# Divided queries and a column of ones in two attentions, and a stream of nine chains on GpSimd and ScalarE in the tail

## The chip, the cores and the metric

The kernel runs on one core of a Trainium2 chip. The metric is the device time of one execution in microseconds; lower is better. The engines are TensorE (PE in the profile; its weight loads are PEld), VectorE (DVE), ScalarE (ACT), GpSimd (POOL) and SyncE (SP), which issues most of the transfers.

## The reference

Four images of 256 channels and 64 x 64 pixels pass four layers, all in float32. Each layer adds its result to its input and begins with a group norm (folded into weights here).

- Layer 0: a pointwise convolution, a depthwise convolution that gives offsets and masks, a deformable sampling of 36 points a pixel (bilinear, from a padded table), a projection, a squeeze-and-excite gate and a feed-forward part of 1024 hidden channels.
- Layer 1: multi-scale linear attention. The part that matters:

```python
qkv = relu(conv1x1(x) * scale + bias)               # 768 channels
agg = conv1x1_dw(conv5x5_dw(qkv))                   # 25 taps a channel
q, k, v = split(concat(qkv, agg))                   # heads of 8 channels; q, k through relu
vk = einsum('bhdn,bhen->bhde', v, k)
out = einsum('bhde,bhen->bhdn', vk, q)
denom = einsum('bhe,bhen->bhn', k.sum(-1), q)
out = out / (denom + EPS)
out = relu(conv1x1(out, proj_w) * scale + bias)
```

- Layer 2: a 3 x 3 convolution with binarised weights, 256 to 256 channels.
- Layer 3: attention whose keys and values come from a 2 x 2 max pool (1024 of them) and whose queries are all 4096 pixels:

```python
m1 = softmax(theta1 @ phi1, axis=2)                 # 4096 x 1024
m2 = m1 @ gi1                                       # 4096 x 128
out = conv1x1(m2, wz_w) + wz_b + x
```

## The kernel before

`run` goes through the images in a pipeline. The sampling of layer 0 is the backbone: `sample(n)` runs 288 rounds for each image, and in each round GpSimd issues four indirect transfers (L591), each of which gathers 256 values for each of 128 partitions into a buffer g of which there are seven. PE multiplies them with the weights wm (L598; wm is made by VectorE at L582), ScalarE copies the accumulator acc to at (L603), PE transposes it (L608), and ScalarE spreads the result (L618).

Beside those rounds a planner, `beside`, advances other generators. Each generator yields the costs of its steps, has a total, and is advanced so that its share of the total follows the share of the rounds. Beside the sampling of image n run the feed-forward part and the linear attention of image n-1 (`feed`, `linear`), and, from n = 2 on, the convolution and the pooled attention of image n-2 (`second`). Within `ordered()` each engine keeps the order in which the program emits instructions; elsewhere a scheduler decides it. After the last sampling comes the tail, where `self.alone` is true: first the feed-forward part, the linear attention of the last image and most of `second(2)`, over 900 planned steps; then the convolution of the last image with the rest of `second(2)`; then the pooled attention of the last image with wider use of PSUM.

Linear attention (`layer1`). `rows` multiplies the qkv weights (L805) in three passes over the image and writes padded rows. There are 24 "chains" an image, each a 5 x 5 depthwise convolution of 128 channels by 16 rows: `aggregate` runs one on VectorE as 25 taps of 128x1024 (L180 for the first, L178) that add up in PSUM; `products` runs one as 25 multiplies on ScalarE (L193, L196 for the first) and 24 additions on GpSimd (L194), with three buffers m between them. `chains` hands the chains out in pairs, ak and av. In the tail chains are taken in threes: the first and the third go to VectorE, the second runs beside them through `aside`, one step in every second tap. `step` is called after each tap in the tail (after every third elsewhere) and runs one closure of the list `later`, which holds all the small steps of the attention. When the last keys and values are in, `summed` masks their products to blocks of 8 (`ln`, L873). `output` makes the denominators (`dens`, L889 to L892), and for each of 8 combinations of half and channel tile `head` multiplies ln with the query (num, L898), spreads the reciprocal denominator over partitions (rden, L901), copies num to ot on ScalarE (L903) and multiplies on VectorE (L904). `proj` multiplies ot with the projection pw (L910), and relu, addition and statistics follow (L912, L913, L110). The constants LINEAR and LAST are the totals that the planner takes for `linear` beside the sampling and in the tail.

The convolution (`layer2`) subtracts and adds its inputs into xd (L987, on GpSimd in the tail), and its products are L1036.

Pooled attention (`layer3`). For each of 32 tiles of 128 queries: two products s (L1135), their maxima mx (L1136, L1137), exp on ScalarE with the sums as a second output (L1142), the sum of the two sums and its reciprocal on VectorE (L1144, L1145), eight transposes (L1150) copied by ScalarE (L1151), eight products with the values gt (L1155), and the scaling by the reciprocal on VectorE into m2 (L1156). Every four tiles a product with ww and the additions follow (L1161 to L1163).

Of the kernel before, what the change touches and what calls it, by code (L numbers as in the profile page):

```python
# [40 lines left out]
FEED = NB * 40 + 8  # L41
LINEAR, LAST = 930, 620
STEPS = 900
# [28 lines left out]
class Net:  # L72
# [675 lines left out]
    def layer1(self, n, st, st2):  # L748
# [3 lines left out]
        with tc.tile_pool(name=f"la{n}", bufs=1, side="right") as sp, \  # L752
# [13 lines left out]

            later, count, aside = [], 0, None
            room = lambda bufs, more=1: bufs + more * self.alone

            def step(cost, chains=False):  # L770


                nonlocal count
                count += chains
                if later and (not self.alone or count % 2 or not chains):
                    later.pop(0)()
                if chains:
                    if count % 8 == 6 if self.alone else count in LEADS:
                        next(made, None)
                    if count % 2 and aside:  # L780
                        next(aside, None)
                return cost
# [59 lines left out]
            def outer(t, kind, kv, vv, first, last):  # L842
# [12 lines left out]
                def added(i):  # L855
                    for j in range(2):
                        nc.tensor.matmul(sums[:, t, kind], kts[i][:, 0, j], kts[i][:, 1, j],
                                         start=first and i + j == 0, stop=last and i + 1 == len(at) and j == 1,
                                         skip_group_check=True)
# [9 lines left out]
            def summed(t):  # L869

                for kind in range(2):
                    j = 2 * kind + t
                    nc.vector.tensor_tensor(ln[:, j], sums[:, t, kind], self.con("bd"), ALU.mult)  # L873
                    kk = sp.tile([P, 1], F32, name=f"kk{j}")
                    nc.vector.tensor_reduce(kk, ks[t][:, kind, 0:(NB, NCH)[kind]], AX.X, ALU.add)
                    for h in range(2):
                        nc.vector.tensor_scalar(ld[:, j, h, 16 * h:16 * h + 16], self.con("oh"), kk, None, ALU.mult)

            def output(c, qp, aq):
# [14 lines left out]
                def head(h, j):  # L894
                    if not j:
                        xv.append(self.block(bp, self.x3_d[n], 2 * c + h, "xq", bufs=1))
                    pn = self.ps("num")
                    nc.tensor.matmul(pn, ln[:, j], qh[h][j], start=True, stop=True)  # L898
                    hs, i = slice(64 * (j // 2), 64 * (j // 2) + 64), 2 * h + j % 2
                    pb = self.ps("rden")  # L900
                    nc.tensor.matmul(pb, self.con("sel")[hs, i * P:(i + 1) * P], rd[0][hs], start=True, stop=True)  # L901
                    ot[h, j] = bp.tile([P, 512], F32, name="ot", tag="kt", bufs=4)
                    nc.scalar.copy(ot[h, j], pn)  # L903
                    nc.vector.tensor_tensor(ot[h, j], ot[h, j], pb, ALU.mult)  # L904

# [46 lines left out]
            def chain():  # L952

                while not (args := next(every)):
                    yield step(3)
                return args

            while number < 6 * NCH:
                count = 0 if not self.alone and number % 2 == 0 else count
                *args, more = yield from chain()  # L960
                if self.alone:

                    *slow, smore = yield from chain()
                    aside = products(*slow, **smore)
                    yield from aggregate(*args, **more)
                    *args, more = yield from chain()
                    yield from aggregate(*args, **more)
                    while next(aside, None):
                        pass
                    number += 3  # L970
                else:
                    yield from aggregate(*args, **more)
                    number += 1
            while later:
# [76 lines left out]
    def layer3(self, n, st, wide=False):  # L1051
        nc, tc, a = self.nc, self.tc, self.a
        M = HW // 4
        with tc.tile_pool(name=f"na{n}", bufs=1, side="left") as sp, \
# [31 lines left out]
            ph = sp.tile([P, M], F32, name="ph")  # L1086
            gt = sp.tile([P, 8, P], F32, name="gt")
            def first(b):
# [15 lines left out]
            def then(b, xq):  # L1104
# [5 lines left out]
                nc.scalar.activation(ph[:, b * P:(b + 1) * P], ps[:, 0:P], AF.Identity, bias=fb)  # L1110
                nc.vector.tensor_tensor(gt[:, b], ps[:, P:2 * P], gb, ALU.add)

# [10 lines left out]
            for b in range(NB):  # L1123
                m2 = bp.tile([P, 512], F32, name="m2")
                for j in range(4):
# [13 lines left out]
                    pe = bp.tile([P, M], F32, name="pe")  # L1139
                    den = bp.tile([P, 3], F32, name="den3")  # L1140
                    for i in range(2):
                        nc.scalar.activation(pe[:, i * 512:(i + 1) * 512], s[i], AF.Exp, bias=mx[:, 2:3], accum_out=den[:, i:i + 1])  # L1142
                    yield 2
                    nc.vector.tensor_tensor(den[:, 2:3], den[:, 0:1], den[:, 1:2], ALU.add)  # L1144
                    nc.vector.reciprocal(den[:, 2:3], den[:, 2:3])  # L1145
                    pT = bp.tile([P, 8, P], F32, name="pT")
# [7 lines left out]
                    for m in range(8):  # L1154
                        nc.tensor.matmul(ps[:, 0:P], pT[:, m], gt[:, m], start=m == 0, stop=m == 7)  # L1155
                    nc.vector.tensor_scalar(m2[:, j * P:(j + 1) * P], ps[:, 0:P], den[:, 2:3], None, ALU.mult)  # L1156
                    yield 3
# [173 lines left out]
```

## Time and profile before

| | |
|---|---|
| three runs | 7739.69, 7744.90, 7749.79 us, median 7744.9 us |
| profiled execution | 7735.88 us, with a span of 7734.1 us |
| mean granted TensorE clock | 0.851 |
| busy of the span: PE, PEld | 5939.0 us (77%), 3468.1 us (45%) |
| busy of the span: VectorE, ScalarE, GpSimd | 5191.6 us (67%), 2200.4 us (28%), 5026.2 us (65%) |
| first and last start of a gather (L591) | 133.2 us, 6250.0 us |
| first and last start of an addition of a chain on GpSimd (L194) | 6549.7 us, 7251.5 us |

A row of the profile gives line, engine, operation, output from inputs and the count; behind the bar come busy time and mean duration of one in ns, and after a second bar the time that the engine sat idle just before such instructions and what ended most of it. A row of waits gives the waiting engine and its operation, what it waited for, the total in us, how many times, and the longest. A matmul in float32 leaves two records. Matmul durations overlap, so their sum is more than the time that PE is held.

### The profile page before, as it was taken

How to read it: one execution, taken by the hardware profiler on the slowest of the kernel's cores; microseconds unless marked ns; L12 is line 12 of the kernel's file. 1: busy time of each engine (PE TensorE's matmuls, PEld its weight loads, DVE VectorE, ACT ScalarE, POOL GpSimd, SP SyncE). 2: the span in 40 equal slices, each digit the busy share in tenths (PEclk: the TensorE clock that was granted, in tenths of full speed). 3: DMA queues.
4: the chain of work that ended last, by engine and by line, in shares of the span. 5: the costliest groups of instructions: out<-in, count | busy, mean ns of one | idle time of the engine just before them, and what ended most of it. 6: DMA issues, size and time to landing. Idle time of an engine off the chain costs nothing. (4 is left out here: it accounts for less than half of the span.)

```text
span 7734.1 us, 94959 instructions
## 1 busy us (share of the span) xinstructions
PE 5939.0 (77%) x36000; PEld 3468.1 (45%) x36000; DVE 5191.6 (67%) x6665; ACT 2200.4 (28%) x4879; POOL 5026.2 (65%) x4870
## 2 busy tenths in 40 slices
PE   5666666579766677898777778987777889967899
PEld 2333333334333333446544434465444435744487
DVE  6555553644787887238888892289888933999634
ACT  1111111212222222223233222222333323655415
POOL 2777777777777777777777667777776621966220
PEclk7676776779777778999898899998888999978999
DMA  6564664565544444555544455465444432210121
GB/s 188 152 178 137 172 173 139 160 183 157 162 122 125 125 141 132 165 151 163 149 144 133 122 154 165 136 170 157 142 134 128 123 123 65 75 52 33 63 87 58
DMA packets 744344, 1031.45 MB, mean 133 GB/s; under 512 B 354128, under 2 KB 459984, under 8 KB 742352
## 3 DMA queue, kind: packets, MB, share of 16 engines
q0 software_dynamic: 221184, 604.27, 27.2%
q1 hardware_dynamic: 522704, 421.10, 18.2%
q8 instruction: 285, 4.67, 0.3%
q14 instruction: 171, 1.40, 0.1%
HBM read 856.39 MB, written 168.61 MB: 133 GB/s over the span
## 5 line engine op out<-in xcount | busy, mean ns | idle before, releaser
L591 POOL DMA_INDIRECT g<-tab,sl x4608 | 4492.3, 975 | 1757.4 <-issue 1273.2
L178 DVE SCALAR_TENSOR_TENSOR agg<-pad,vec,agg 128x1024 f32<-128x1024 f32 x2280 | 2934.0, 1287 | 60.6
L598 PE MATMUL acc<-g,wm 128*32 128x128 f32 x18432 | 1266.6, 319 | 1241.6 <-ACT at L603 711.0
L598 PEld LDWEIGHTS acc<-g,wm 128*32 128x32 f32 x18432 | 623.2, 121 | 1927.9 <-ACT at L603 951.2
L1036 PE MATMUL ps<-xd,w 128*128 128x256 f32 x3072 | 712.3, 385 | 7.3 <-DVE x L1016 2.8
L582 DVE TENSOR_TENSOR wm<-con,sl 128x768 f32<-128x768 f32 x384 | 365.8, 953 | 420.3 <-PE acc L598 400.7
L1036 PEld LDWEIGHTS ps<-xd,w 128*128 128x128 f32 x3072 | 577.6, 193 | 107.3 <-issue 29.8
L618 ACT COPY dT<-dp 64x128 f32<-64x128 f32 x1152 | 296.7, 258 | 1044.3 <-PE dp L608 705.6
L730 PE MATMUL ps<-x2f,f 128*128 128x512 f32 x1024 | 479.0, 615 | 4.0 <-ACT f L705 4.0
L740 PE MATMUL ps<-hm,f 128*128 128x512 f32 x1024 | 462.0, 600 | 0.0
L715 DVE SCALAR_TENSOR_TENSOR hm<-ps,vec,lk 128x512 f32<-128x512 f32 x256 | 192.2, 751 | 400.4 <-ACT lk L732 397.3
L805 PE MATMUL ps<-xr,qw 128*128 128x512 f32 x768 | 450.7, 718 | 11.5 <-DVE ot L904 4.1
L987 POOL TENSOR_TENSOR xd<-xp 128x640 f32<-128x640 f32 x64 | 79.5, 1269 | 477.3 <-ACT xp L999 382.9
L603 ACT COPY at<-acc 128x256 f32<-128x256 f32 x576 | 214.4, 372 | 490.0 <-PE acc L598 477.9
L732 ACT ACTIVATE lk<-ps,low 128x512 f32<-128x512 f32 x256 | 175.9, 687 | 594.9 <-PE ps L730 593.6
L631 PE MATMUL po<-dT,ow 128*128 128x288 f32 x1024 | 312.2, 455 | 13.4 <-ACT dT L626 6.5
L608 PE MATMUL dp<-ident,at 128*128 128x128 f32 x1152 | 267.6, 320 | 66.8 <-ACT dT L618 54.7
L194 POOL TENSOR_TENSOR ak<-ak,m 128x1024 f32<-128x1024 f32 x96 | 228.1, 2376 | 131.0 <-ACT m L193 126.7
L1155 PEld LDWEIGHTS ps<-gt,pT 128*128 128x128 f32 x2048 | 278.5, 215 | 60.7 <-issue 34.3
L1155 PE MATMUL ps<-gt,pT 128*128 128x128 f32 x2048 | 291.0, 302 | 7.1 <-ACT pT L1151 7.0
L730 PEld LDWEIGHTS ps<-x2f,f 128*128 128x128 f32 x1024 | 191.3, 194 | 230.1 <-issue 216.9
L194 POOL TENSOR_TENSOR av<-av,m 128x1024 f32<-128x1024 f32 x96 | 226.9, 2363 | 101.1 <-ACT m L193 96.7
(246 smaller groups left out, 7723.0 us busy)
## 6 DMA issues: line engine op xcount, KB each, us to landing
g<-tab,sl POOLq DMA_INDIRECT x4608
x<-x SPq DMA_DIRECT2D x128, 512.0 KB
xr<-x SPq DMA_DIRECT2D x96, 512.0 KB
tab<-xo SPq DMA_DIRECT2D x192, 128.0 KB
x<-in_x SPq DMA_DIRECT2D x32, 512.0 KB
y<-yc SPq DMA_DIRECT2D x32, 512.0 KB
yb<-y SPq DMA_DIRECT2D x64, 256.0 KB
x<-yb SPq DMA_DIRECT2D x64, 256.0 KB
```

Of the source, the lines that this page charges most:

```text
L178: nc.vector.scalar_tensor_tensor(to, s, wt, acc, ALU.mult, ALU.add)
L194: nc.gpsimd.tensor_tensor(acc, acc, m, ALU.add)
L582: nc.vector.tensor_tensor(wm, self.con("own").unsqueeze(1).unsqueeze(1).to_broadcast(sh), blocks[b][:, r:r + WR, G:].unsqueeze(3).to_broad ...
L591: nc.gpsimd.indirect_dma_start(out=g[:, i, :], out_offset=None, in_=table, in_offset=bass.IndirectOffsetOnAxis(ap=sl.bitcast(I32)[:, r, i: ...
L598: nc.tensor.matmul(acc[32 * i:32 * i + 32, :], wm[:, r4, 4 * i + 2 * x:4 * i + 2 * x + 2, :], g[:, i, x * P:(x + 1) * P], start=x == 0, st ...
L618: nc.scalar.copy(dT[b][hs, :, r:r + UR], dp[u][hs, :, :, s, :].rearrange("p v g o -> p g v o"))
L631: nc.tensor.matmul(po[m][:, 0:BR * OB], self.ow[:, k, m * P:(m + 1) * P], dT[b][:, k].rearrange("p r o -> p (r o)"), start=k == 0, stop=k ...
L730: nc.tensor.matmul(ps, f1[:, k, m * P:(m + 1) * P], x2[:, k], start=k == 0, stop=k == KT - 1)
L740: nc.tensor.matmul(ps, f2[:, k, m * P:(m + 1) * P], hm[:, k], start=k == 0, stop=k == 4 * KT - 1)
L805: nc.tensor.matmul(ps, qw[:, k, m * P:(m + 1) * P], x[:, k], start=k == 0, stop=k == KT - 1)
L1036: nc.tensor.matmul(ps[:, e], w[:, k, t, 2 * half + e, m * P:(m + 1) * P], v[:, 2 * half + e, k, t:t + 8], start=i % 6 == 0, stop=i % 6 == 5)
L1155: nc.tensor.matmul(ps[:, 0:P], pT[:, m], gt[:, m], start=m == 0, stop=m == 7)
```

## The change

It has four parts. In linear attention the two matrices that the query passes, ln and the projection, are multiplied once in `summed` (comb), the product takes the place of pw, and `head` divides the query itself: num and its copy are gone. In pooled attention the values get a 129th column of ones, so that the product gives the sums of the exponentials too; exp has no second output, VectorE takes the reciprocal from the product's last column, and ScalarE does the scaling. In the tail nine of 24 chains, not eight, go to GpSimd and ScalarE, as a stream of their own (`others`) that takes the next chain whenever it has ended one and advances 9/15 of a step for each tap on VectorE. LAST is 580 for 620.

```diff
-LINEAR, LAST = 930, 620
+LINEAR, LAST, ASIDE = 930, 580, 9
...
                 if chains:
                     if count % 8 == 6 if self.alone else count in LEADS:
                         next(made, None)
-                    if count % 2 and aside:
-                        next(aside, None)
+                    if aside:
+                        due += ASIDE / (6 * NCH - ASIDE)
+                        while due > 1:
+                            next(aside, None)
+                            due -= 1
                 return cost
...
-                        nc.tensor.matmul(sums[:, t, kind], kts[i][:, 0, j], kts[i][:, 1, j],
+                        nc.tensor.matmul(sums[:, t, kind], kts[i][:, 1, j], kts[i][:, 0, j],
...
             def summed(t):
 
+                pc = self.ps("comb").rearrange("p (e o) -> p e o", e=2)
                 for kind in range(2):
...
+                for kind in range(2):
+                    nc.tensor.matmul(pc[:, kind], ln[:, 2 * kind + t], pw[:, 2 * kind + t], start=True, stop=True)
+                    nc.vector.tensor_copy(pw[:, 2 * kind + t], pc[:, kind])
...
-                    pn = self.ps("num")
-                    nc.tensor.matmul(pn, ln[:, j], qh[h][j], start=True, stop=True)
...
-                    nc.scalar.copy(ot[h, j], pn)
-                    nc.vector.tensor_tensor(ot[h, j], ot[h, j], pb, ALU.mult)
+                    nc.vector.tensor_tensor(rw(ot[h, j]), qh[h][j], rw(pb), ALU.mult)
...
+            def others():
+
+                for _ in range(ASIDE):
+                    while not (args := next(every)):
+                        yield
+                    *args, more = args
+                    yield from products(*args, **more)
+
+            if self.alone:
+                aside, number = others(), ASIDE
             while number < 6 * NCH:
                 count = 0 if not self.alone and number % 2 == 0 else count
                 *args, more = yield from chain()
-                if self.alone:
-
-                    *slow, smore = yield from chain()
-                    aside = products(*slow, **smore)
-                    yield from aggregate(*args, **more)
-                    *args, more = yield from chain()
-                    yield from aggregate(*args, **more)
-                    while next(aside, None):
-                        pass
-                    number += 3
-                else:
-                    yield from aggregate(*args, **more)
-                    number += 1
+                yield from aggregate(*args, **more)
+                number += 1
+            if aside:
+                for _ in aside:
+                    pass
...
-            gt = sp.tile([P, 8, P], F32, name="gt")
+            gt = sp.tile([P, 8, P + 1], F32, name="gt")
+            nc.vector.memset(gt[:, :, P:], 1.0)
...
-                    den = bp.tile([P, 3], F32, name="den3")
                     for i in range(2):
-                        nc.scalar.activation(pe[:, i * 512:(i + 1) * 512], s[i], AF.Exp, bias=mx[:, 2:3], accum_out=den[:, i:i + 1])
+                        nc.scalar.activation(pe[:, i * 512:(i + 1) * 512], s[i], AF.Exp, bias=mx[:, 2:3])
                     yield 2
-                    nc.vector.tensor_tensor(den[:, 2:3], den[:, 0:1], den[:, 1:2], ALU.add)
-                    nc.vector.reciprocal(den[:, 2:3], den[:, 2:3])
...
-                        nc.tensor.matmul(ps[:, 0:P], pT[:, m], gt[:, m], start=m == 0, stop=m == 7)
-                    nc.vector.tensor_scalar(m2[:, j * P:(j + 1) * P], ps[:, 0:P], den[:, 2:3], None, ALU.mult)
+                        nc.tensor.matmul(ps[:, 0:P + 1], pT[:, m], gt[:, m], start=m == 0, stop=m == 7)
+                    rden = bp.tile([P, 1], F32, name="rden")
+                    nc.vector.reciprocal(rden, ps[:, P:P + 1])
+                    nc.scalar.activation(m2[:, j * P:(j + 1) * P], ps[:, 0:P], AF.Copy, scale=rden)
```

More of the change, by code (lines that the diff above doesn't have):

```diff
@@ L765, in layer1 @@
             nc.vector.memset(ld, 0.0)
-            later, count, aside = [], 0, None
+            later, count, aside, due = [], 0, None, 0
             room = lambda bufs, more=1: bufs + more * self.alone
             def step(cost, chains=False):
-                nonlocal count
+                nonlocal count, due
                 count += chains
@@ L1110, in then @@
                 nc.scalar.activation(ph[:, b * P:(b + 1) * P], ps[:, 0:P], AF.Identity, bias=fb)
-                nc.vector.tensor_tensor(gt[:, b], ps[:, P:2 * P], gb, ALU.add)
+                nc.vector.tensor_tensor(gt[:, b, 0:P], ps[:, P:2 * P], gb, ALU.add)
             xq = None
```

## The prediction

> **What bounds the kernel now.** I read the share of each engine first, then the 40 slices, then busy times by stretch, then who waits in each stretch, and last the groups of single stretches.
>
> ```profile
> POOL 2777777777777777777777667777776621966220
> L591 POOL DMA_INDIRECT g<-tab,sl x4608 | 4492.3, 975 | 1757.4 <-issue 1273.2
> L178 DVE SCALAR_TENSOR_TENSOR agg<-pad,vec,agg 128x1024 f32<-128x1024 f32 x2280 | 2934.0, 1287 | 60.6
> ```
>
> GpSimd is level at 7 until slice 32. Those are the 4608 gathers of the sampling: 0.95 us each and 0.30 us of issue ("issue" 318.4 us over 1045 times in the third image), so 1.25 us, and 1152 of them for an image are 1440 us. Up to 6258 us the gathers set the time, unless they are held up. The waits of GpSimd for PE, by image (second, third, fourth; from the waits of 1540:3040, 3000:4620 and 4600:6258), say where they are:
>
> ```profile
> POOL g L591 <- PE acc L598: 21.0, 16, 4.6
> ...
> POOL g L591 <- PE acc L598: 119.4, 72, 7.6
> ...
> POOL g L591 <- PE acc L598: 114.1, 67, 6.7
> ```
>
> In the second image linear attention alone runs beside the sampling and little is lost. In the third and fourth the convolution and the pooled attention of an earlier image run too, and about 98 + 93 us are lost. Most of it lies where pooled tiles and the output of linear attention overlap. Below are two stretches of the third image, then the tail (columns: stretch, length, busy PE, PEld, DVE, ACT, POOL):
>
> ```profile
> 3860.00:4240.00 380.00, 269.31 (x2179) 183.96 (x2178) 337.17 (x407) 136.94 (x339) 280.20 (x293) 0.88 0.48 138
> 4240.00:4560.00 320.00, 247.13 (x1605) 142.39 (x1604) 272.57 (x334) 100.07 (x241) 199.07 (x207) 0.87 0.42 123
> ...
> 6548.00:6775.00 227.00, 216.60 (x1040) 175.78 (x1040) 217.84 (x245) 142.72 (x190) 201.79 (x98) 0.99 0.25 69
> 6775.00:7000.00 225.00, 149.00 (x596) 100.78 (x595) 214.81 (x259) 132.94 (x198) 144.81 (x61) 0.80 0.15 49
> 7000.00:7253.00 253.00, 200.26 (x674) 106.27 (x673) 235.74 (x277) 137.35 (x207) 138.75 (x60) 0.89 0.12 40
> 7253.00:7345.00 92.00, 83.67 (x330) 46.81 (x330) 39.02 (x83) 35.46 (x69) 0.86 (x1) 0.99 0.21 73
> 7345.00:7530.00 185.00, 182.94 (x863) 159.04 (x862) 55.88 (x124) 25.71 (x38) 39.56 (x32) 1.00 0.31 92
> 7530.00:7734.00 204.00, 190.00 (x1040) 145.17 (x1040) 94.69 (x253) 103.35 (x232) 0.00 (x0) 0.98 0.17 57
> ```
>
> In 4240:4560 a gather takes 320/207 = 1.55 us; VectorE is busy 85%, PE 77%. From 6548 to 7253 VectorE is busy 668.4 of 705 us: the tail's linear attention is bound by VectorE, its first third by PE too (216.6 of 227). From 7253 on PE bounds.
>
> ```profile
> L1144 DVE TENSOR_TENSOR den<-den 128x1 f32<-128x1 f32 x21 | 20.9, 997 | 0.0
> L1156 DVE TENSOR_SCALAR m<-ps,den 128x128 f32<-128x128 f32 x21 | 7.2, 345 | 0.8 <-PE ps L1155 0.8
> ...
> L194 POOL TENSOR_TENSOR ak<-ak,m 128x1024 f32<-128x1024 f32 x96 | 228.1, 2376 | 131.0 <-ACT m L193 126.7 <-DVE agg L178 0.6
> L194 POOL TENSOR_TENSOR av<-av,m 128x1024 f32<-128x1024 f32 x96 | 226.9, 2363 | 101.1 <-ACT m L193 96.7
> L987 POOL TENSOR_TENSOR xd<-xp 128x640 f32<-128x640 f32 x26 | 32.5, 1271 | 0.0
> ```
>
> These are groups of 6548:7253. An add of one element a partition (L1144) takes 997 ns there, though its median over the run is 154.
>
> **What the Trainium skill says.** "SBUF — State Buffer", section "SBUF: two separate sides": VectorE with two SBUF inputs and a GpSimd operation that reads SBUF share a port pair as an exclusive lock held for the whole instruction. The 997 ns beside GpSimd's 2.37 us adds, and about 147 ns beside the gathers (2.20 us for 15 in 4240:4560), agree. "GPSIMD Engine Reference", section 4.1, calls GpSimd about 2x slower on two-input operations: here 2.37 us against VectorE's 1.287 us for a tap, 1.84x, with ScalarE's multiply (L193, 1157 ns) on top. "TensorE: Matmul & The Clock Gate", section "Architectural detail", has ACT and DVE as strict first-in-first-out: an operation that waits holds all behind it. The trace agrees: in 4240:4560 ScalarE waits 55.6 us for mx of L1137, and PE 49.1 us for ScalarE's copies at L603.
>
> **The change, part by part.**
>
> *Divided queries.* For each of 128 heads (32 an image) the product num (two matmul records of 0.43 us of PE, the pace of L910 on the timeline) and ScalarE's copy (586 ns) go; VectorE's multiply (680 ns) stays and takes the query for the copy. So PE loses 27.5 us an image, ScalarE 18.8, VectorE nothing. In exchange pw is multiplied by ln once: four comb products an image (0.43 us each for two records, at half the width) and four copies of 128x256 (423 ns, as L1019). VectorE waits for PE between them; bounds 0.5 us (the hop) to 5 us (PE waiting for a gather), I take 1. Behind it wait taps; in the second to fourth images' sampling VectorE has room for that at this point, in the tail it costs about 6 us with the copies. No DMA and no SP instruction is added or moved in number.
>
> *Column of ones.* For each of 32 tiles an image VectorE loses the den add and the scaling (345 ns) and keeps a reciprocal, now from PSUM (164 ns from SBUF; bounds 150 to 350). ScalarE loses two accumulator reads (197 ns each) and gains the scaling of 128x128 from PSUM (368 ns, the row of L1110): about even. The product gets 129 columns for 128: 1.78 us a tile becomes 1.794. A slower odd width can't be excluded; bound 10%, 6 us in the last stage. The new wait: ScalarE's scaling waits for VectorE's reciprocal, and behind it on ScalarE are the at copies, exp, and the multiplies for GpSimd.
>
> *Sampling.* In 4240:4560 VectorE loses 15 x (0.147 + 0.345) = 7.4 us, PE 32 x 0.43 = 13.8, ScalarE 9.4. Of VectorE's 47 us idle I take 8 to go, as its waits for rden, ps and pr (31 us) stand behind shorter PE work. That gives 15 us of the 61 above 207 x 1.25. In 3860:4240 only 14 us are above 293 x 1.25, and 16 x 0.5 = 8 us leave VectorE: 5. The fourth image repeats the third, the first and second gain nothing (gathers cover it): **-40 us**; bounds 0 and -110, and below nothing by the rival on ScalarE.
>
> *Tail, nine of 24 chains.* VectorE loses a chain, 24 x 1.284 + 1.336 = 32.2 us, and in 6548:7253 21 den adds (20.9) and 21 scalings (7.2): 60.3, less 6 for comb: 54. GpSimd gains 24 x 2.37 = 57 us: 455 + 57 + 32.5 = 545 of some 660, still under VectorE; ScalarE 29 + 7.7 - 12.9 - 8.7 = +15. GpSimd's chain adds now stand up to six, not five, ahead of each pair of xd (L987), at most 2.4 us more for the convolution, which works a block ahead: nothing. The instruction order has 148 taps on VectorE, not 159, before the last statistics of conv(2): 11 of the 25 removed taps, 14 us, fall where PE is the bound too, and I count 5 of them. 54 - 9 = 45, and 5 off for ScalarE and GpSimd out of step: **-40 us**; bounds -60 and 0.
>
> *7253 to 7345.* Ten num products leave PE (8.6 us), but 13 heads instead of 11, and 8 additions at L913 instead of 6, come after the last tap: **-3**. *Last stage:* 0.5 us for the columns; in the new PE order, about a dozen times only the product (1.78 us) stands between the second half of s and the transposes that need its exp (2.75 before), and that chain takes 1.91 on the timeline: 1.6 us; at the very end VectorE and ScalarE for VectorE alone, 0.3: **+3** rounded, up to +10. conv(3), 7345 to 7530, is PE's and unchanged.
>
> Sum: -40 - 40 - 3 + 3 = **-80 us**, from the profiled execution's 7735.9 to 7656. The median of the runs shown is 9 us above that execution, so 7744.9 - 80 = **7665 us**.
>
> **Rivals.**
>
> *ScalarE waits for rden (slower).* Place: 64 tiles beside the gathers and 21 in the tail. For: VectorE runs behind there, and the like wait for mx costs ScalarE 55.6/15 = 3.7 us a tile. Against: ScalarE has just been brought level with VectorE by mx, and seven gather buffers lie between PE and GpSimd. It decides above (80 + 15)/85 = 1.1 us a tile; at half of 3.7 it costs 157 us: 7744.9 + 77 = **7822 us**. 9%.
>
> *Half lands.* In the tail GpSimd, busy 89% already in 6548:6775, becomes the bound with ScalarE (gain 0 to 10), or the sampling is held by PE's waits for at and keeps its 40. For: 0.6 GpSimd steps a tap need 1.42 us beside 1.28. Against: other VectorE work of over 0.4 us a tap. **7705 us**, 20%.
>
> *More lands.* The gather waits of the third and fourth image fall by 110 rather than 40, and the tail gives 55: **7580 us**. For: a queue just over its limit (1.25 us a gather against 272.6/207 = 1.32 of VectorE) frees up steeply. Against: convolution and group norm lose there too and are untouched. 14%.
>
> *It does not do what it says.* VectorE still multiplies every head, so "lighter" touches engines with room, and the ninth chain only moves the bound: within 15 us of **7745 us**, 5%. Against: taps of VectorE in the tail are 375 for 400 in the instruction order.
>
> **How the numbers follow.** The forecast case has 52%, its own range is 7630 to 7695. With most of "half" and half of "more" the range is 7600 to 7730; left out are the slower rival, part of no change and the far end. A change of 0.2%, 15 us, is about what a measurement of this kernel can tell from none: faster 0.52 + 0.20 + 0.14 = 0.86, same 0.05, slower 0.09.
>
> **What would show it.** Right: waits of L591 for acc in the third and fourth images near 100 us each; the chain stage some 665 us long with VectorE over 93% busy and GpSimd about 545 us; last stage 204 to 210 us. Wrong: ScalarE waiting over 1 us a tile for rden with PE's wait for at longer; GpSimd over 95% in the chain stage; the tile's product above 1.9 us.

## The result, and the profile after

The changed kernel takes 7822.6 us (median of four runs, 7819.5 to 7826.5), the kernel before 7746.4 us (four runs, 7739.7 to 7749.8): **slower, ratio 1.0097 [1.0084, 1.0110], +76 us**. 7665 us was forecast, with a range from 7600 to 7730 us.

The profiled span is 7817.7 us for 7734.1. From the page of the changed kernel (the slices of GpSimd, then two groups: busy us, mean ns, idle before):

```profile
POOL 2777777777777777767777667777776612976220
...
L591 POOL DMA_INDIRECT g<-tab,sl x4608 | 4506.5, 978 | 1785.2 <-issue 1263.5
L178 DVE SCALAR_TENSOR_TENSOR agg<-pad,vec,agg 128x1024 f32<-128x1024 f32 x2257 | 2904.0, 1287 | 61.2
```

GpSimd idles longer before its gathers (1785 us for 1757), and a gather is as long as it was: nothing was gained in the sampling. The taps on VectorE are fewer, as meant, by 30 us. The waits of the second image, then of the third, then of the fourth (total us, times, longest):

```profile
POOL g L591 <- PE acc L598: 21.6, 19, 4.6
...
POOL g L591 <- PE acc L598: 138.4, 79, 11.3
ACT m L1162 <- DVE rden L1161: 134.8, 32, 15.3
...
ACT pe L1148 <- DVE mx L1144: 89.4, 22, 7.8
...
POOL g L591 <- PE acc L598: 132.5, 80, 8.9
ACT m L1162 <- DVE rden L1161: 132.0, 32, 12.9
```

The gathers wait 138 and 132 us for PE in the third and fourth images, where before they waited 119 and 114 and where 100 was to show the forecast right. The new wait of ScalarE for rden is 267 us over 64 tiles, 4.2 us a tile. By stretches (length, busy PE, PEld, DVE, ACT, POOL, granted clock): two stretches beside the gathers, the chain stage, the output after the last tap, the convolution, and the last stage:

```profile
3860.00:4240.00 380.00, 268.78 (x2152) 182.38 (x2152) 327.69 (x372) 136.00 (x318) 280.32 (x288) 0.87 0.47 136
4240.00:4560.00 320.00, 235.72 (x1498) 137.44 (x1498) 256.78 (x295) 90.99 (x204) 194.46 (x201) 0.84 0.41 120
6545.00:7309.00 764.00, 591.01 (x2414) 406.03 (x2412) 639.32 (x770) 450.19 (x613) 545.39 (x246) 0.86 0.18 55
7309.00:7405.00 96.00, 82.66 (x285) 42.60 (x284) 37.29 (x62) 28.99 (x47) 4.91 (x3) 0.95 0.16 55
7405.00:7605.00 200.00, 190.01 (x885) 164.33 (x884) 57.14 (x131) 29.78 (x41) 39.52 (x32) 0.97 0.32 97
7605.00:7818.00 213.00, 194.02 (x1043) 145.98 (x1041) 81.36 (x189) 107.30 (x200) 0.00 (x0) 0.97 0.16 55
```

VectorE, GpSimd and PE all work less in 4240:4560, yet 201 gathers pass in it for 207. In the chain stage VectorE is busy 639 of 764 us, 84%, where over 93% was forecast: it lost work and waits instead. GpSimd's 545 us are as forecast.

To compare kernels I cut each span at the same events: the last gather, the last matmul of the feed-forward part (L740), VectorE's last tap, the last relu of the projection, the convolution's last matmul, and the end of the span (us):

| kernel | last gather | feed | chain | output | convolution | last stage |
|---|---|---|---|---|---|---|
| before | 6250.0 | 255.7 | 747.1 | 78.7 | 197.9 | 204.7 |
| after | 6292.0 | 253.2 | 764.2 | 96.3 | 199.4 | 212.6 |
| e1 divided queries | 6272.2 | 254.2 | 738.8 | 75.3 | 199.0 | 206.2 |
| e2 column, ScalarE scales | 6291.1 | 257.2 | 733.7 | 79.1 | 202.0 | 212.9 |
| e8 column, VectorE scales | 6256.2 | 255.7 | 741.1 | 78.3 | 197.9 | 212.8 |
| e3 stream of nine | 6264.1 | 257.1 | 763.4 | 114.9 | 202.3 | 205.5 |
| e5 stream of eight | 6259.3 | 256.0 | 762.8 | 97.1 | 197.0 | 205.1 |

From before to after: +42 us in the sampling, +35 in the chain and output stages of the tail, +8 in the last stage. The two profiled executions lie 84 us apart, 7 more than the medians, since that of the kernel before was 10 us under its median. The last gather varies by some 14 us where no code beside it was changed (6250 before, 6259 and 6264 in e5 and e3), so a few us there are not a finding. Each row is one profiled execution.

### The profile page after: what moved, and what is told of

Read it like the earlier page. It is cut to its first block, busy times and chain, and to the rows that moved or that the text cites. A ratio compares the mean times of both kernels' runs of the same rounds, so it can differ in the third digit from the quotient of the medians.

```text
span 7817.7 us, 94070 instructions
## 1 busy us (share of the span) xinstructions
PE 5936.8 (76%) x35776; PEld 3482.4 (45%) x35776; DVE 5114.1 (65%) x6404; ACT 2174.8 (28%) x4648; POOL 5097.0 (65%) x4894
## 3 DMA queue, kind: packets, MB, share of 16 engines
q14 instruction: 167, 1.37, 0.1%
## 5 line engine op out<-in xcount | busy, mean ns | idle before, releaser
L178 DVE SCALAR_TENSOR_TENSOR agg<-pad,vec,agg 128x1024 f32<-128x1024 f32 x2257 | 2904.0, 1287 | 61.2
L598 PE MATMUL acc<-g,wm 128*32 128x128 f32 x18432 | 1296.1, 323 | 1237.2 <-ACT at L603 703.7
L740 PE MATMUL ps<-hm,f 128*128 128x512 f32 x1024 | 462.0, 600 | 0.0
L194 POOL TENSOR_TENSOR av<-av,m 128x1024 f32<-128x1024 f32 x144 | 341.6, 2372 | 137.3 <-ACT m L193 129.7
L1159 PE MATMUL ps<-gt,pT 128*128 128x129 f32 x2048 | 296.1, 305 | 6.6 <-ACT pT L1155 6.4
L1142 PE MATMUL s<-ph,th 128*128 128x512 f32 x512 | 275.4, 651 | 20.1 <-DVE r L1169 7.4
## 6 DMA issues: line engine op xcount, KB each, us to landing
yb<-y SPq DMA_DIRECT2D x64, 256.0 KB
x<-yb SPq DMA_DIRECT2D x64, 256.0 KB
```

Of the source, the lines that this page charges most:

```text
L178: nc.vector.scalar_tensor_tensor(to, s, wt, acc, ALU.mult, ALU.add)
L194: nc.gpsimd.tensor_tensor(acc, acc, m, ALU.add)
L598: nc.tensor.matmul(acc[32 * i:32 * i + 32, :], wm[:, r4, 4 * i + 2 * x:4 * i + 2 * x + 2, :], g[:, i, x * P:(x + 1) * P], start=x == 0, st ...
L740: nc.tensor.matmul(ps, f2[:, k, m * P:(m + 1) * P], hm[:, k], start=k == 0, stop=k == 4 * KT - 1)
L1142: nc.tensor.matmul(s[i], tv[:, 4 * b + j], ph[:, i * 512:(i + 1) * 512], start=True, stop=True)
L1159: nc.tensor.matmul(ps[:, 0:P + 1], pT[:, m], gt[:, m], start=m == 0, stop=m == 7)
```

## The experiments

**The parts, each alone** (e1 to e3), and the change with the scaling back on VectorE (e4). The edits are those of the change; e4 differs from the changed kernel in

```diff
-nc.scalar.activation(m2[:, j * P:(j + 1) * P], ps[:, 0:P], AF.Copy, scale=rden)
+nc.vector.tensor_scalar(m2[:, j * P:(j + 1) * P], ps[:, 0:P], rden, None, ALU.mult)
```

> The kernel before with the divided queries alone (comb in summed, num and its copy gone). Theory W (the loss is ScalarE's new in-order wait for rden in pooled attention): this part has no such wait, so it gains: 10 to 40 us, 7705 to 7735 us, and the gathers end before 6250 us. Theory S (the loss is the tail's stream): the same. Theory Q (fewer steps on PE and ScalarE change nothing where VectorE sets the pace): 7740 to 7750 us.

> The kernel before with the column of ones alone, the scaling on ScalarE. Theory W: ScalarE waits some 4 us a tile for rden, and this part alone is slower by 50 to 90 us, 7795 to 7835 us, 50 us or more of it before the last gather. Theory S: this part is neutral or gains, 7715 to 7750 us.

> The kernel before with the tail's stream of nine chains alone (ASIDE 9, LAST 580). Theory W: the tail gains the VectorE chain of 32 us as forecast, less what is out of step: 7705 to 7735 us. Theory S: the part while conv(2) runs beside it is bound by GpSimd, ScalarE and PE, and it loses 15 to 35 us: 7760 to 7780 us.

> The changed kernel with one edit: the scaling by rden goes back to VectorE, right behind the reciprocal, so ScalarE has no wait for rden; the column of ones stays. Theory W: the gathers end at or before 6250 us, and the total is at or below the kernel before, 7680 to 7750 us. Theory S: only some 10 us better than the changed kernel, 7800 to 7820 us.

Measured, beside 7748.0 us: e1 7742.2 us, ratio 0.9996 [0.9989, 1.0003]; e2 7776.9, 1.0032 [1.0021, 1.0044]; e3 7802.3, 1.0069 [1.0052, 1.0086]; e4 7806.5, 1.0072 [1.0056, 1.0089]. e1 lies in the range of theory Q and e4 in that of S; e2 loses less than W expected, but more than S allows, and e3 loses more than either theory expected. Two parts lose and one gives nothing clear of noise; the tail's stream is the largest loss. The sum, -6 + 29 + 54 = +77, is near the measured +76, but e4 shows that the parts act on each other: in the changed kernel the scaling on VectorE is worth 16 us (7806.5 for 7822.6), and alone it is worth 36, as the next run shows.

**The column with the scaling left on VectorE** (e8: e2 with the line of e4).

> The kernel before with the column of ones alone, but the scaling left on VectorE behind the reciprocal. With the scaling on ScalarE the column costs 29 us: 8 in the last stage, the rest mostly before the last gather. Theory W (ScalarE's wait for rden): the part before the last gather goes, the last stage stays 213 us: 7750 to 7762 us. Theory C (the column, its later reciprocal or its wider product is at fault): 7770 to 7780 us.

7740.7 us, ratio 0.9990 [0.9983, 0.9997], less than even theory W expected. e2 and e8 differ only in the engine that scales, and by 36 us; 35 of them lie before the last gather (6291 for 6256), 0.55 us for each of 64 tiles. Waits from 3000 us to the last gather, of e2 and then of e8:

```profile
PE acc L598 <- ACT at L603: 452.9, 207, 12.6
...
POOL g L591 <- PE acc L598: 264.0, 139, 9.8
...
ACT m L1156 <- DVE rden L1155: 210.4, 64, 10.5
...
ACT pe L1142 <- DVE mx L1138: 157.8, 42, 5.8
```

```profile
PE acc L598 <- ACT at L603: 425.7, 192, 12.1
...
POOL g L591 <- PE acc L598: 241.4, 144, 9.8
...
ACT pe L1142 <- DVE mx L1138: 225.4, 42, 15.9
```

ScalarE waits 210 us for rden, 3.3 us a tile, but 68 us of its waits for mx are gone: part of the new wait stands in the place of the old one. What remains goes on through PE, which waits 27 us longer for the at copies of ScalarE, to the gathers, which wait 23 us longer for PE. In the changed kernel the same step is smaller: between it and e4 the last gather moves by 15 us (6292.0 and 6277.3). And with the scaling on VectorE the parts alone would sum to -6 - 7 + 54 = +41 us, where e4 has +58; what they do to each other I did not separate.

**The form of the stream** (e5 to e7; all have the stream alone). e5 is `ASIDE = 8`, `LAST = 620`, so that only the form differs from before; e6 is `ASIDE = 9`, `LAST = 620`; e7 is e3 with

```diff
-if later and (not self.alone or count % 2 or not chains):
+if later and (not self.alone or count % 2 or len(later) > 8 or not chains):
```

> The kernel before with the stream form but eight chains (ASIDE 8, LAST 620). The stream with nine costs 54 us in the run before this: 16 between the feed-forward part and the last tap, 36 from the last tap to the last relu of the projection. Theory N (the ninth chain is too much for GpSimd and ScalarE and leaves too few taps): eight as a stream are like before, 7740 to 7755 us. Theory F (the form, chains handed out as they come, is at fault): 7775 to 7805 us, the stretch after the last tap again above 100 us.

> The stream of nine alone, with LAST 620 as before instead of 580, so the chains run ahead of the convolution and the pooled tiles at the pace of before. Theory P (LAST 580 slows the linear attention against its companions): better than the 7802 us of the stream alone, 7760 to 7780 us. Theory N: no better, 7795 to 7825 us, as GpSimd has more to do for each convolution block.

> The stream of nine alone, with one edit in step: a closure of later is also run at even taps when more than eight wait. Theory D (a closure runs at every second tap, so 25 taps fewer leave 13 heads instead of 10 behind the last tap): the stretch after the last tap falls from 115 us towards 80 us, total 7765 to 7780 us. Theory N: the closures only move earlier and lengthen the stretch before: total within 10 us of 7802 us.

Beside 7747.4 us: e5 7777.0 us, 1.0039 [1.0027, 1.0050]; e6 7798.0, 1.0063 [1.0047, 1.0080]; e7 7803.1, 1.0072 [1.0055, 1.0089]. So LAST is not the cause, and running the closures earlier (in the tail one runs at every second tap) only moves the loss (chain stage 801 us, output 76). The form loses 30 us with the same work; the ninth chain, which was to take 32 us from VectorE, loses 21 more (e6) or 25 (e3). Chain and output together, of before and then of e5 (columns as above):

```profile
6505.70:7331.50 825.80, 676.99 (x2733) 447.51 (x2732) 718.55 (x901) 463.62 (x691) 493.64 (x224) 0.90 0.18 56
```

```profile
6515.30:7375.20 859.90, 699.67 (x2747) 458.52 (x2746) 720.40 (x902) 464.16 (x692) 493.76 (x224) 0.87 0.17 54
```

VectorE, ScalarE and GpSimd are busy for the same time; VectorE idles 139.5 us for 107.3, and PE takes 23 us more for the same matmuls, at a granted clock of 0.87 for 0.90. VectorE's waits there, before and then e5:

```profile
DVE ot L904 <- PE rden L901: 18.8, 14, 2.5
...
DVE m L1156 <- PE ps L1155: 4.9, 5, 1.2
```

```profile
DVE ot L907 <- PE rden L904: 33.2, 18, 4.2
...
DVE m L1161 <- PE ps L1160: 16.4, 13, 4.2
```

VectorE meets PE's results later than before, in linear attention's output and in the pooled tiles. 480 us after the end of the feed-forward part the two kernels have begun 257 and 256 taps of L178; e5 falls behind only after that, in the part with the output. Two things differ: a side chain of the stream is closed only in its 26th advance, which also begins the next chain, and this puts the output two taps later in VectorE's order (93 taps after the first den of the tail in e5, 95 before); and the side chain runs on over the ends of main chains.

**What the two taps cost.** From here on the runs met chips on which the kernel before itself takes 8716 to 8804 us: the sampling takes some 950 us longer there, for all kernels, while the tail is much the same. I read these runs by the ratio to before on the same chip and by their tail. Before has no profile there; e12 and e16 have e1's program in the tail and take 819.2 and 818.3 us for chain and output where e1 took 814.1, so before's 825.8 would be about 831 there, an estimate. It is a rough one: e13, e17 and e18 below have the same instructions in the tail and take 804.8, 817.2 and 807.6 us.

e9 and e15 are one kernel, the stream of eight with each side chain closed in its 25th advance:

```diff
-yield from self.products(...)
-end(out, done, relu, **more)
+for t, cost in enumerate(self.products(...), 1):
+    if t == 25:
+        end(out, done, relu, **more)
+    yield cost
```

e14 is the kernel before with an empty closure ahead of each output:

```diff
+if self.alone:
+    later.append(lambda: None)
 later.append(dens)
```

> The stream with eight chains, as before, but each side chain is closed (its relu and what follows it queued) in the same advance as its 25th step, not in a 26th. Then VectorE's order of instructions is exactly that of the kernel before, and only 19 multiplies of ScalarE, 3 additions of GpSimd and some 20 TensorE rows stand elsewhere. Theory 'order': the 30 us that the stream of eight lost (7777) come from what the 26th advance does: linear attention's output stands two taps later in VectorE's order, against the tiles of pooled attention. Then the time is that of before, 7740 to 7755 us, with VectorE's idle time between the end of the feed and the last pr back at about 110 us (142 in the stream of eight). Theory 'stream': a side chain that runs on over the ends of main chains costs in itself: about 7777 us, and idle time at about 140.

> The kernel before with one edit in the tail: an empty entry ahead of each chunk's output in the queue of closures, so that linear attention's output stands two taps later in VectorE's order (the first den 93 taps before the last one, as in the stream of eight, for 95 before). Theory 'order': this alone gives most of the loss of the stream of eight, ratio 1.002 to 1.005 (15 to 40 us), with VectorE idle 130 us or more from the end of the feed to the last pr. Theory 'stream': the output's place is of no account: ratio 0.999 to 1.001.

> The stream of eight chains closed in the 25th advance, as in e9, beside e14 on one chip. Theory 'order': ratio 0.999 to 1.0015, since VectorE's order is that of before. Theory 'stream': 1.003 to 1.005, as the stream of eight with its 26th advance (1.0039).

| kernel | ratio | chain, output, us | sum, us | VectorE idle in it, us |
|---|---|---|---|---|
| before | 1 | 747.1, 78.7 (first chips) | about 831 (estimate) | 107 (of 825.8, first chips) |
| e9 / e15 | 1.0015 [1.0003, 1.0028] / 1.0012 [1.0002, 1.0023] | 758.1, 78.6 / 757.9, 78.6 | 836.8 / 836.5 | 118 / 118 |
| e14 | 1.0020 [1.0008, 1.0032] | 750.8, 96.0 | 846.8 | 126 |
| e5 (first chips) | 1.0039 [1.0027, 1.0050] | 762.8, 97.1 | 859.9 | 140 |

The delay of the output (two taps for the first two outputs, four for the third in e14) costs about 16 us by the estimate (846.8 against 831) and 7 to 28 by the ratio: more than "stream" expected, less than "order" expected of VectorE's idle time (126 us, not 130). It is seen in the output stage, where the spread is small: all profiled kernels that keep the output where before has it take 73 to 79 us there, e14 and e5 96 and 97. So the 18 us that e5 loses in the output are the delay's, as far as profiles of different chips can show it. Without the delay e9 and e15 still lose 0.12 to 0.15%, some 6 us of it in the tail by the estimate, though the order of VectorE's instructions is that of before, memsets apart; e15 lies in the range of "order", e9 a little above its own. In e9 a wait of PE is longer (10.2 us; 2.1 in e5):

```profile
PE pt L857 <- POOL av L194: 10.2, 3, 5.2
```

PE's transposes of a side chain wait for GpSimd's last additions, since the chain is closed an advance earlier. The other half of e5's 34 us, 16 us in the chain stage, is in none of these runs alone; I did not separate it.

**The ninth chain.** e10 is the stream of nine with e9's edit; e11 is e10 with the chains spread unevenly:

```diff
-due += ASIDE / (6 * NCH - ASIDE)
+due += 1 / 2 if number < ASIDE + 6 else 2 / 3
```

> The stream with nine chains as in the changed kernel, alone, with each chain closed in its 25th step. Theory 'GpSimd is late': nine chains ask 0.6 of a step for each tap, 1.42 us of GpSimd for 1.29 of VectorE, so GpSimd falls behind from the start, and PE, whose transposes of that chain come in its order right after the chain's end, waits for GpSimd's last addition, the convolution's chains behind it. Closing two taps earlier doesn't help that: 7790 to 7810 us (7802 without). Theory 'order': the loss is that of the 26th advances: 7730 to 7765.

> As the run before it (nine chains, closed in the 25th step), but the nine chains are spread unevenly: half a step for each tap over the first six main chains, two thirds over the last nine, where VectorE has the output and the tiles to do as well and a tap comes each 1.6 to 2 us. Theory 'GpSimd is late': the first 300 us of the stage run as before (150 taps in about 270 us from the end of the feed, 300 with the even spread), PE's waits for av in the tail fall under 8 us (19.6 in the even stream), and the ninth chain pays: 7725 to 7755 us. If GpSimd's rate in the first third isn't what costs, the time stays within 10 us of the run before it.

e10 1.0071 [1.0053, 1.0090], as 'GpSimd is late' expected; chain and output 881.6 us (e3 878.3). e11 1.0047 [1.0030, 1.0065], 852.3 us. Half a step for each tap at the start, in place of 0.6, is worth 29 us of the tail by the profiles, and 19 us by the medians of all executions (8755.4 for 8774.3). PE's waits for side chains in the two stages, of e3, e10 and e11:

```profile
PE pt L854 <- POOL av L194: 19.6, 3, 11.5
...
PE pt L857 <- POOL av L194: 32.0, 4, 14.2
...
PE pt L857 <- POOL av L194: 11.2, 3, 5.3
```

What goes wrong at 0.6 is seen in the timeline of e3 some 120 us after the end of the feed-forward part; first GpSimd, then PE, then VectorE (start us, length, engine, line, operation, count, and in brackets the idle time before it):

```profile
6637.19 4.77 POOL L194 TENSOR_TENSOR av<-av,m 128x1024 f32<-128x1024 f32 x2
...
6642.02 0.48 PE L854 MATMUL pt<-ident,av 128*128 128x128 f32 x1 [11.51 <-POOL av L194]
6642.29 0.42 PE L853 MATMUL pt<-ident,ak 128*128 128x128 f32 x1
6642.50 0.42 PE L854 MATMUL pt<-ident,av 128*128 128x128 f32 x1
6642.71 2.63 PE L1041 MATMUL ps<-xd,w 128*128 128x256 f32 x6
...
6648.39 0.69 DVE L1021 TENSOR_TENSOR x<-x,ps 128x512 f32<-128x512 f32 x1 [7.86 <-PE ps L1041]
```

GpSimd ends a side chain at 6641.96. PE has stood 11.5 us at the transposes of that chain, with the convolution's products behind them in its order, and VectorE has waited 7.9 us for those when it gets its operand; in these 7.9 us no tap runs. From 6581 to 6641 us GpSimd is busy 58.7 of 60 us in e3. 300 us after the end of the feed-forward part e3 has begun 141 taps of L178, e10 138, e11 148 and before 158. From 120 to 270 us after it, before does 96 taps, the first ones of chains counted: 1.56 us a tap. There GpSimd, at 0.6 of a step for each tap, would need 1.37 us a tap (24 additions of 2.37 us in 25 steps), and for the convolution's xd (21.6 us in that stretch) 0.22 more: 1.59 us, an estimate. So at before's pace GpSimd has no room for the ninth chain there. That the rate is the cause is supported by the fall of PE's waits, but not isolated, as e11 also moves the output (70 taps follow its first den, 80 in e10). And the expected 7725 to 7755 us of e11 (at most 1.001) was missed: its waits of PE for av are still 11.2 us, where under 8 was expected, and the output still takes 102.8 us after the last tap. Beside e9, with eight chains, the ninth chain makes the chain stage 8.5 us shorter (749.6 for 758.1) and the output 24 us longer.

**Divided queries, and what num covers.** e12 and e16 are one kernel, e1 with num still made beside the gathers, unread:

```diff
+if not self.alone:
+    nc.tensor.matmul(self.ps("num"), ln[:, j], qh[h][j], start=True, stop=True)
```

e13 and e17 are one kernel too; they join that to the column scaled on VectorE, with the old denominator (sums of exp, 128 columns) in the last stage and triples in the tail. e18 is the same without num.

> Divided queries alone, but beside the gathers the product num is still made in its old place (into a PSUM tile that nothing reads), so PE's count of matmuls there is that of before, while ScalarE's copies stay gone; in the tail it is gone. Divided queries alone took 7742 us, with the end of the gathers at 6272 against 6250 to 6258, at a lower granted clock in the stretches with pooled tiles (0.79 to 0.87 for 0.84 to 0.91 from 4200 to 4600 us), and 11 us less in the tail. Theory 'cover': those products were what PE did while VectorE made rd; without them PE stands still there and is granted a lower clock, which slows the other matmuls. Then the clock in these stretches is back at 0.88 to 0.91, the gathers end at 6245 to 6258, and the time is 7725 to 7737 us. Theory 'nothing to gain': PE's work there is neither a cost nor a cover: 7738 to 7750, gathers' end at 6260 to 6275.

> As e12: divided queries, with the product num still made beside the gathers. Theory 'cover': granted clock in the stretches with pooled tiles back at 0.88 to 0.91, gathers' end at 6245 to 6258 where before's is 6250, ratio 0.997 to 0.999. Theory 'nothing to gain': gathers' end at 6260 to 6275, ratio 0.9990 to 1.0005.

> The parts that can gain, put together: divided queries (with num still made beside the gathers, as a cover for PE), the column of ones with the scaling left on VectorE, and in the last stage the old denominator (sums of exp, 128 columns); the tail in triples as before. If 'cover' is right: divided -6 alone and another -10 to -15 beside the gathers, column on VectorE -7 alone and its 8 us in the last stage back: 7715 to 7730 us, ratio 0.996 to 0.998. If the num products are no cover and the last stage's 8 us are not the column's: 7733 to 7745, ratio 0.998 to 1.000.

> As e13: divided queries with num still made beside the gathers, column of ones scaled on VectorE, the old denominator in the last stage, triples in the tail. Theory 'cover': ratio 0.9965 to 0.9980, and at least 0.0008 below the run without num (e18); granted clock from 60% of the span to the end of the gathers at or above that run's, by 0.01 to 0.04. Theory 'nothing to gain': the two within 0.0005 of each other, or this one above.

> As e17, but without num anywhere. Theory 'cover': ratio 0.9980 to 0.9995, with the gathers' end 8 us or more later than in e17. Theory 'nothing to gain': 0.9965 to 0.9985 like e17, gathers' end within 6 us of e17's.

e12 1.0005 [0.9990, 1.0021]; e16 0.9992 [0.9982, 1.0003]; e13 0.9978 [0.9967, 0.9990]; e17 0.9967 [0.9953, 0.9980]; e18 0.9947 [0.9929, 0.9965]. The theory came from e1. Two stretches with pooled tiles, of before and of e1:

```profile
4200.00:4600.00 400.00, 311.01 (x2029) 176.69 (x2032) 346.49 (x421) 126.53 (x306) 257.25 (x268) 0.88 0.45 133
5900.00:6200.00 300.00, 235.19 (x1446) 120.52 (x1446) 263.61 (x302) 89.89 (x214) 189.74 (x196) 0.90 0.42 124
```

```profile
4200.00:4600.00 400.00, 302.11 (x1987) 182.45 (x1988) 342.07 (x419) 116.50 (x288) 255.79 (x266) 0.83 0.43 126
5900.00:6200.00 300.00, 235.49 (x1448) 130.69 (x1441) 259.18 (x303) 80.06 (x196) 187.13 (x195) 0.83 0.42 125
```

Without num the granted clock is 0.83 for 0.88 and 0.90, and over all executions its mean is 0.835 in e1 and 0.848 in before. PE's busy time over the whole span falls by 18 us only (5921.2 for 5939.0) where 110 us of num were removed and 7 of comb added, by the prediction's durations. This looked like a saving eaten by the clock, but the other pair says otherwise: from e17 to e18 PE's busy time falls by 66 us (5955.7 to 5889.3) where 96 heads, 83 us, are gone; and two profiles of one kernel, e13 and e17, lie 56 us apart (5899.9, 5955.7). So how much the clock takes back is not shown.

Before has no profile on these chips, so what was expected of its last gather and clock can't be compared. By their ratios alone e12 and e16 fit "nothing to gain" and e13 and e17 fit "cover". The pair e17 and e18, on one chip, decides against "cover", which wanted e17 the faster one by 0.0008 or more. The median of e18, without num, is 23 us lower (8755.5 us, e17 8778.8); the intervals overlap, so that e18 is faster is not clear of noise, and neither theory expected 0.9947. In the profiles e18's last gather is 37 us earlier (7259.2, 7296.4), but the profiled e17 was 15 us above its median and the profiled e18 9 us below. Yet e18's clock is lower again, 0.795 for 0.804 over all executions (3200:3700 and 5200:5700, of e17 and then of e18):

```profile
3200.00:3700.00 500.00, 323.32 (x1881) 138.03 (x1882) 334.94 (x334) 75.00 (x197) 318.81 (x331) 0.73 0.40 116
5200.00:5700.00 500.00, 387.66 (x2113) 182.23 (x2112) 245.53 (x288) 99.14 (x230) 305.97 (x314) 0.84 0.44 133
```

```profile
3200.00:3700.00 500.00, 301.88 (x1826) 135.51 (x1826) 336.69 (x338) 77.08 (x203) 326.21 (x336) 0.67 0.41 117
5200.00:5700.00 500.00, 368.88 (x2068) 178.99 (x2060) 241.68 (x285) 100.00 (x230) 311.06 (x320) 0.81 0.46 137
```

The Trainium skill, "TensorE: Matmul & The Clock Gate", section "Part 1: The HAM clock gate", has a block that watches how busy PE is and sets its clock by that; the means here, lower where PE has less to do, agree. But a lower clock goes with less work on PE, and it is no proof of lost time. That holds for the chip of this pair, one with the long sampling; on those of e1 the pair wasn't run, so what cost e1 its gain before the last gather stays open. One thing is seen there: from 3000 us to the last gather, ScalarE's wait for mx is 278.2 us in e1 for 219.6 before, and the gathers' wait for PE 248.3 for 233.5. Part of the time that ScalarE had spent on the copies of num, and on its waits for num (204.6 us before), became a longer wait for VectorE.

e18 is faster than the kernel before by 0.53% [0.35%, 0.71%]; it keeps the two light parts, leaves out what lost, and was measured on one chip only. Its tail (chain and output 807.6 us) is 23 us under the estimate for before; the parts on the first chips sum to -18 (e1 -12, e8 -6). Its last stage, without the column, takes 204.7 us, as in before, where e2 and e8 take 212.9 and 212.8: the column of ones costs the last stage its 8 us, whoever scales.

## Why the prediction was wrong

*Sampling, -40 us.* Wrong, +42 measured. The step that failed is "That gives 15 us of the 61": it took 7.4 us of work removed from VectorE, and 8 us of its idle time "to go", as time for the gathers, one for one. On the first chips divided queries (last gather 6272) and the column on VectorE (6256) gave nothing beside before's 6250. In e1 what the removed work left was filled by waits: ScalarE's for mx, +59 us. The main case also put the new wait for rden at nothing; it is 4.2 us a tile. Of the 42 us it explains about 15 (e4); the 22 us of e1 stay open.

*Rival, "ScalarE waits for rden".* Right in mechanism and side: 36 us between e2 and e8, 16 between the changed kernel and e4. Its price was too high: it took half of 3.7 us a tile on the path. The wait is 3.3 us in e2 (4.2 in the changed kernel), a third of it replaces the wait for mx, and 0.55 us a tile reaches the gathers in e2 (0.23 in the changed kernel). It alone didn't decide the sign, as the terms that were to outweigh it (-80) were not there. That the total of this rival, 7822 us, is the measured one is luck: the tail makes up nearly half of the loss, and the rival has the tail gaining.

*Tail, -40 us.* Wrong in sign: the stream alone is +54, of which 52.5 us are in the chain and output stages. Two steps failed. First, "545 of some 660, still under VectorE": 545 us are right, but as a mean over a stage with different limits. Early in the stage GpSimd needs some 1.59 us a tap for VectorE's 1.56, so it has no room, and PE stands up to 11.5 us (14.2 in e10) at its late chains. The rival "half lands" named the rate (1.42 us, xd left out of it) and stopped at a gain of nothing; since PE takes its work in order, the late chain holds the convolution too. e11 supports this step, as far as said there. Second, the stream's form was costed at nothing: closed in the 26th advance, a chain moves the output by two taps, some 18 of the 34 us that the form loses in the tail (e14); what the other 16 are is open. The order was read for counts of taps, not for where the output stands against the pooled tiles.

*7253 to 7345, -3 us.* Wrong, +17.6 for the output. Without the ten num products, priced at 8.6 us, this stage is 3.4 us shorter (e1 alone: 75.3 us for 78.7). What failed is the price of "13 heads instead of 11, and 8 additions at L913 instead of 6", which was 8.6 - 3 = 5.6 us: the stream alone adds 18 us there with eight chains and 36 with nine. In the trace of before 10 heads follow the last tap, not 11; the 13 and the 8 came as counted.

*Last stage, +3 us, up to +10.* Right in kind, and mis-sized: 7.9 us. The 129th column costs 0.6 us, as argued; the products before, then after:

```profile
L1155 PE MATMUL ps<-gt,pT 128*128 128x128 f32 x512 | 62.7, 276 | 0.5 <-ACT pT L1151 0.5
```

```profile
L1159 PE MATMUL ps<-gt,pT 128*128 128x129 f32 x512 | 63.3, 276 | 0.5 <-ACT pT L1155 0.5
```

The wait that was named for the new order of PE is there: the transposes' loads wait 6.1 us for exp, 0.6 before. The term of 1.6 us for it was too small. A second one was not named: s (weight loads and products) waits 8.2 and 4.2 us for mx where before waited 2.9 and 0.8.

*What was right.* Most counts and durations, GpSimd's and ScalarE's loads in the tail, and the convolution as unchanged (199.4 us for 197.9).

## What to carry to other kernels

Work removed from one engine is worth only what the engine that ends last had been waiting for: show that wait ahead of the forecast, or take the gain as nothing. Compare rates stretch by stretch where two engines must keep step, with all that the slower one has in its queue; a mean over the stage hides a start in which it can't keep up. When a loop of steps is rewritten, look in which advance each piece is closed: one advance later moved the output by two taps, which alone costs about as much as either light part saves in the tail.

## What the runs showed that was not expected

- The granted clock fell when products that nothing depended on were left out, 0.804 to 0.795 (e17 and e18, the means of all executions), and the kernel was not slower.
- Two profiles of one kernel on two chips can differ by 56 us in PE's busy time (e13 and e17).
- A late output, with the same instructions, made the stage after the last tap 17 us longer (96.0 us in e14, 73 to 79 where it is not late).
- The same kernel took 7747 us on some chips and 8716 to 8804 on others; nearly all of the added time lies before the last gather (7191 to 7296 us for 6250 to 6292, over all kernels), and chain and output differ by about 5 us for one program (e1 814.1, e12 and e16 819.2 and 818.3).
